# Ordering the last three groups of a two-layer graph network kernel: softmax one pair ahead, seeded first results, another share-out of the tails

## The chip, the cores and the metric

The kernel runs on one core of one Trainium2 chip. The metric is the device time of one launch in microseconds (us). The time before is the median of three runs. Beside it stands one profiled execution, whose span (first to last instruction) is what the trace is read in.

## The reference

Inputs: `x` of 128 batches x 128 tokens x 512 features, float32, an adjacency matrix `adj` (128 x 128), weights for one attention layer. Cut to what matters:

```python
# layer 0: a max over neighbours, through two einsums with the same adj
A = einsum('od,bdn->bon', adj, x);  C = A + b
x = layernorm(x + max(relu(A[:, :, None, :] + (C - A)[:, :, :, None]), axis=-1))
# layer 1: masked attention with 8 heads of 64 features, mask where adj == 0
q, k, v = split(x @ w_qkv)
p = softmax(where(adj == 0, -inf, q @ k.T * 64 ** -0.5))
o = (p @ v) @ w_proj + b_proj
x = layernorm(x + o + layernorm(o) * gamma + beta)
```

So each batch of 128 tokens passes a small matmul and a maximum, a layernorm, a q/k/v projection, scores, a softmax over 8 x 128 x 128 values, attention, an output projection, and then a "tail": an inner layernorm of o, two additions, and an outer layernorm.

## The kernel before, in words

**Tiling.** Four batches make a group (NG = 32 groups), and batches are handled in pairs (64 pairs, loop variable p). The projections of a group (512 tokens x 512 features) are done by a scheme with 7 products instead of 8 block products: operands are added up beforehand (`left_sums`, `weight_sums`) and the 7 products are combined afterwards. Class `Unit` does this for q/k of a half (`qk_unit`), for v (`v_unit`) and for the output projection (`o_unit`). A product is four matmuls of 128 x 256, each of which shows as two records in the trace. It accumulates in one of four PSUM banks b1 to b4: products 1, 6, 7 in b1, product 2 in b2, products 5 and 3 in b3, product 4 in b4. `snap(k)` copies b1 to SBUF on ScalarE after products 1, 6 and 7. `result(half, col)` adds a bank and a snap on VectorE and so makes one quarter of the output: (0,0) from b2 and snap 1, (0,1) from b3 after product 3 and snap 2, (1,0) from b4 and snap 3, (1,1) from b3 before product 3 and snap 3. Product 3 can therefore start only when (1,1) was read, and the next unit's product 5 only when (0,1) was read.

**Softmax.** `scores(b)` writes eight heads to two PSUM tiles (tags pss0 and pss1, or po and pa). `softmax_max` scales and masks them into an SBUF tile `s` (two buffers) and takes the maximum on VectorE; `softmax_exp` runs eight exponentials with sums on ScalarE; `softmax_div` divides on VectorE; `prob_transpose` transposes 32 x 32 blocks on VectorE. `prob_write` sends the result to DRAM (`hop`), and `prob_read` fetches it back with rows regrouped (`pT`, two buffers, four transfers of 128 KB), both on SyncE's (SP's) queue. `prob_move` is the three in a row. `attend(b)` multiplies with v; `attend_copy` moves the result to `oT`.

**Tails.** In the loop a pair's tail is: bias on GpSimd (`tail_bias`), statistics on VectorE (`bn_stats`, `bn_aggr`), power -0.5 on GpSimd (`finish_stats`), inner layernorm on ScalarE (`tail_inner`), three operations on GpSimd (`tail_residual`: times gamma, plus o, plus the spilled x), outer statistics, outer layernorm on ScalarE (`tail_outer`) and the store. Behind the loop this is done batch by batch (`tail_inner_one`, `tail_residual_one`, `tail_outer_one`). For some batches VectorE does it instead of GpSimd (`fused_open`, `fused_close`), and for some batches ScalarE makes the outer statistics (`scalar_stats`, `finish_scalar_stats`). The last group's projection is not a Unit: `last_project` multiplies each batch by all of w_proj into a bank that `last_seed` filled with the bias.

**What sets the order.** Everything is pinned in program order (`keep_in_program_order`), so each engine runs its instructions in the order in which the text issues them. A wait holds whatever is queued behind it on that engine. SP's queue carries all transfers of this part.

**Around the change.** With L = 127 the last batch, the loop runs p up to LAST = 60. Iteration 60 attends batches 118 and 119 (L-9, L-8) and starts the softmaxes of L-7 and L-6. What follows the loop is written out by hand: o of group 29, v of group 31 and o of group 30 (in the text `o_u`, `v_u`, `o_u`), the softmaxes of L-5 to L, the tails of the last 14 batches, and the four last projections. In that part o units are seeded with the bias (`seed`, a ScalarE copy into banks 2, 3 and 4).

Of the kernel before, what the change touches and what calls it, by code (L numbers as in the profile page):

```python
# [16 lines left out]
def kernel(  # L17
# [144 lines left out]
    class Unit:  # L162
# [25 lines left out]

        def result(self, half, col):
            bank, k = {(0, 0): (2, 1), (0, 1): (3, 2), (1, 0): (4, 3), (1, 1): (3, 3)}[half, col]  # L190
            pin(
                nc.vector.tensor_tensor(  # L192
                    self.out[half, col], self.banks[bank], self.snaps[k], ALU.add
                )
            )
# [55 lines left out]
    def finish_stats(mv, keys, eng=None, fused=0):  # L251

        n = len(keys)
        if n == 0:
            return
        sh = small.tile([P, NC], F32, tag="sh", name=f"sh_{mv.name}")
        if eng is None:
            pin(nc.vector.tensor_scalar(sh[:, :n], mv[:, :n, 0], -1.0, None, ALU.mult))
# [3 lines left out]
        if eng is None:  # L262
            tt(nc.gpsimd, sh[:, :n], sh[:, :n], rs[:, :n], ALU.mult)
        elif n > fused:

            part = slice(fused, n)
            pin(eng.tensor_scalar(sh[:, part], mv[:, part, 0], -1.0, None, ALU.mult))
            tt(eng, sh[:, part], sh[:, part], rs[:, part], ALU.mult)
# [232 lines left out]
    def o_unit(g):  # L501
# [4 lines left out]
        return Unit(f"o_{g}", o_lefts[g], tokens_stationary(wp), out)  # L506
# [11 lines left out]

    def seed(unit, bank):
        cols = slice(HE, D) if bank == 3 else slice(0, HE)  # L520
        bias = bp_bc[:, cols].unsqueeze(1).to_broadcast([P, 2, HE])
        pin(nc.scalar.copy(unit.new_bank(bank), bias))
# [37 lines left out]
    def tail_reload_one(b, place):  # L560
        rs_[b] = place
        pin(nc.sync.dma_start(out=place, in_=spill[b // 2][:, b % 2]))
# [71 lines left out]
    def stats(name, *items, eng=None, fused=0):  # L634

        mv = small.tile([P, NC, 2], F32, tag="mv", name=f"mv_{name}")
        for k, (kind, b) in enumerate(items):
            bn({"o": o_of, "z": zs.get, "y": xs.get}[kind](b), mv, k)
        finish_stats(mv, items, eng, fused)
        return mv  # L640
# [131 lines left out]
    for p in range(LAST + 1):  # L772
# [121 lines left out]
        elif p == LAST:  # L894
            second = qk_unit(g + 1, 1)
# [23 lines left out]
        if p == 1:  # L919
            weight_sums(wp, 0, HE)  # L920
        if f is not None:
            one("y", xs, f)
# [6 lines left out]

    L = B - 1  # L930
    po_pa = ("po", "pa")
    pool = nc.gpsimd
# [4 lines left out]
    before.snap(3)  # L937
    attend_copy(L - 7)
    attend(L - 6, "pa")
    attend_copy(L - 6)  # L940
    seed(o_u, 2)
    scores(L - 5)
    scores(L - 4, po_pa)
    before.result(1, 1)
    tail_inner(B // 2 - 7)
    softmax_max(L - 5)
    before.result(1, 0)
    softmax_max(L - 4)
    o_u.product(1)
    o_u.snap(1)  # L950
    o_u.product(2)
    softmax_exp(L - 5)
    seed(o_u, 4)
    o_u.result(0, 0)
    before.product(3)
    before.result(0, 1)
    tail_residual(B // 2 - 7)
    softmax_exp(L - 4, range(4))
    o_u.product(6)
    scores(L - 3)  # L960
    scores(L - 2, po_pa)
    o_u.snap(2)
    seed(o_u, 3)
    softmax_exp(L - 4, range(4, H))
    softmax_div(L - 5)
    prob_move(L - 5)
# [3 lines left out]
    softmax_max(L - 3)  # L970
    softmax_exp(L - 3, range(4))
    o_u.snap(3)
    softmax_exp(L - 3, range(4, H))
    softmax_div(L - 4)
    prob_move(L - 4)
    softmax_max(L - 2)
    o_u.result(1, 1)
    o_u.result(1, 0)
    tail_outer(B // 2 - 8)
    tail_store(B // 2 - 8)  # L980
    tail_reload(B // 2 - 6)
    wlast, room = last_load()
    for t in range(L - 9, L + 1):
        tail_reload_one(t, room[:, t - L + 9])
    v_u.product(2)
    v_u.product(1)
    v_u.snap(1)
    stats("last_1", ("o", L - 9), ("o", L - 8), eng=pool)
    softmax_exp(L - 2, range(4))
    o_u.product(3)  # L990
    o_u.result(0, 1)
    v_u.result(0, 0)
    v_u.product(6)
    v_u.snap(2)
    softmax_exp(L - 2, range(4, H))
    for t in (L - 9, L - 8):
        tail_inner_one(t)
    tail_residual_one(L - 9)
    v_u.product(5)
    v_u.product(7)  # L1000
    stats("last_2", ("o", L - 11), ("o", L - 10), eng=pool)
    tail_residual_one(L - 8, [0])
    softmax_div(L - 3)
    prob_transpose(L - 3)
    prob_write(L - 3)
    v_u.snap(3)
    v_u.product(4)
    v_u.result(1, 1)
    softmax_div(L - 2)
    prob_transpose(L - 2)  # L1010
    prob_write(L - 2)


    attend(L - 5)
# [5 lines left out]
    scores(L - 1)  # L1020
    scores(L, po_pa)
    run_sums(o_sums(NG - 2))
    o_u = o_unit(NG - 2)
    seed(o_u, 2)
    for t in (L - 11, L - 10):
        tail_inner_one(t)
    softmax_max(L - 1)
    v_u.result(1, 0)
    v_u.product(3)
    softmax_max(L)  # L1030
    softmax_exp(L - 1, range(4))
    o_u.product(1)
    o_u.snap(1)
    seed(o_u, 4)
    softmax_exp(L - 1, range(4, H))
    v_u.result(0, 1)
    o_u.product(2)
    seed(o_u, 3)
    o_u.product(6)
    o_u.snap(2)  # L1040
    o_u.result(0, 0)
    softmax_exp(L, range(4))
    tail_residual_one(L - 8, [1, 2])
    stats("last_3", ("z", L - 13), ("z", L - 12), ("z", L - 9), eng=pool)
    o_u.product(5)
    o_u.product(7)
    softmax_exp(L, range(4, H))
    o_u.snap(3)
    o_u.product(4)
    softmax_div(L - 1)  # L1050
    prob_move(L - 1)
    o_u.result(1, 1)
    softmax_div(L)
    prob_move(L)
    tail_residual_one(L - 11)
    tail_residual_one(L - 10)
    tail_outer(B // 2 - 7)
    tail_store(B // 2 - 7)
    tail_outer_one(L - 9)
    last_seed(L - 3, "b2")  # L1060
# [3 lines left out]
    attend_copy(L - 2)  # L1064
    o_u.result(1, 0)
    mv = small.tile([P, NC, 2], F32, tag="mv", name="mv_last_4")
# [111 lines left out]
```

## Time and profile before

| | before |
|---|---|
| runs, us | 1964.82, 1963.43, 1963.56 |
| median, us | 1963.56 |
| profiled execution, us | 1965.37 |
| its span, us | 1963.5 |
| mean granted TensorE clock | 0.995 |
| start of iteration 60 on TensorE | 1840.79 |
| last matmul of the trace starts | 1946.5 |
| stores and loads on SP's queue, 1838 to 1964 | 19.68 MB |

Names of engines: PE is TensorE (matmuls), PEld its weight loads, DVE VectorE, ACT ScalarE, POOL GpSimd, SP SyncE. In the rows "L74" is a line of the kernel; every matmul has L74, and every two-input elementwise operation made by the helper `tt` has L77, so rows are told apart by the tiles: `b_qk`, `b_v`, `b_o` the banks of a unit, `pss` scores, `po`/`pa` attends, `pp` last projections, `s` softmax tile, `pu` its transpose, `hop` and `pT` its way through DRAM, `u_*` snaps, `zl` and `z` tails, `mv_last` mean and variance, `rs_mv_last` and `sh_mv_last` scale and shift made of them, `wlast` the tile that holds w_proj and the reloaded x of the last batches. A number after an operation on a timeline is start and duration in us. The profiled execution is one run; its rows give durations.

### The profile page before, as it was taken

The page shows a single profiled execution, that of the slowest core. Times are in us where ns is not written, and L with a number is a line of the kernel's source. Part 1 is how long each engine was busy: PE and PEld are TensorE (multiplying, and loading weights), DVE is VectorE, ACT ScalarE, POOL GpSimd, SP SyncE. Part 2 cuts the span into 40 slices and gives each one's busy share as a digit, 9 for nine tenths or more (in the row PEclk, how much of TensorE's full clock was granted, in tenths as well). Part 3 has the DMA queues.
Part 4 walks back from the last instruction along what each step waited for, and adds up shares of the span by engine and source line. Part 5 has one row for each costly group of instructions (what it writes and reads, how often), then busy time and mean ns, then how long its engine had stood idle before and what let it go on. Part 6 is the DMA issues. An engine that isn't in the chain of part 4 may idle for free.

```text
span 1963.5 us, 33034 instructions
## 1 busy us (share of the span) xinstructions
PE 1935.3 (99%) x11533; PEld 1637.7 (83%) x11533; DVE 1561.6 (80%) x2513; ACT 1061.6 (54%) x3084; POOL 1297.2 (66%) x827
## 2 busy tenths in 40 slices
PE   9999999999999999999999999999999999999995
PEld 6888888888888888888888888888888888888873
DVE  6767878878778778788787787787887877877876
ACT  3444654655555546546555555455465555554564
POOL 6336766767666767667676667676676766676748
PEclk9999999999999999999999999999999999999998
DMA  7647557576576676675675765765756657667554
GB/s 226 171 119 189 148 175 193 156 189 173 166 196 163 167 200 161 171 186 163 188 181 161 195 162 167 207 156 168 193 158 187 175 169 193 166 168 194 141 182 139
DMA packets 445653, 341.73 MB, mean 174 GB/s; under 512 B 276912, under 2 KB 378416, under 8 KB 445488
## 3 DMA queue, kind: packets, MB, share of 16 engines
q1 hardware_dynamic: 445056, 338.85, 63.3%
q8 instruction: 91, 1.49, 0.3%
q10 hardware_dynamic: 432, 0.79, 0.1%
q14 instruction: 74, 0.61, 0.1%
HBM read 172.82 MB, written 166.72 MB: 173 GB/s over the span
## 4 chain that ended last, share of the span: by engine, by line
PE 96%; DVE 2%; POOL 1%; ACT 1%; DMA 1%; issue 0%; SPq 0%; POOLq 0%; DVEq 0%; ACTq 0%
PE b_qk L74 40%; PE b_v L74 19%; PE b_o L74 18%; PE pss L74 6%; PE po L74 6%; PE pa L74 5%; PE pp L74 0%; DMA wlast<-spill 0%; ACT s L420 0%; POOL zl L77 0%; DVE s L401 0%; DVE s L77 0%; POOL rs_mv_last L77 0%; DVE st_mv_last L248 0%; DVE pu L441 0%
## 5 line engine op out<-in xcount | busy, mean ns | idle before, releaser
L74 PE MATMUL b_qk<-s_x,wqk 128*128 128x256 f32 x2048 | 473.2, 379 | 0.2 <-DVE v L192 0.2
L74 PEld LDWEIGHTS b_qk<-s_x,wqk 128*128 128x128 f32 x2048 | 389.0, 190 | 54.1 <-DVE v L192 0.6
L420 ACT ACTIVATE s<-s,nmax 128x128 f32<-128x128 f32 x1024 | 396.2, 391 | 5.7 <-DVE nmax L413 5.7
L74 PE MATMUL b_qk<-x1T,wqk 128*128 128x256 f32 x1536 | 358.9, 383 | 0.1
L74 PEld LDWEIGHTS b_qk<-x1T,wqk 128*128 128x128 f32 x1536 | 286.6, 190 | 45.3 <-issue 1.0
L77 POOL TENSOR_TENSOR z<-z,ga_bc 128x1024 f32<-128x1024 f32 x58 | 164.7, 2839 | 169.2 <-ACT z L274 169.2
L260 POOL TENSOR_SCALAR rs_mv<-mv 128x6 f32<-128x6 f32 (+2 forms) x61 | 14.6, 239 | 380.9 <-DVE mv L249 380.9
L77 DVE TENSOR_TENSOR s<-s,rec 128x1024 f32<-128x1024 f32 x128 | 252.0, 1969 | 4.4
L186 ACT COPY u_qk<-b_qk 128x512 f32<-128x512 f32 x192 | 112.4, 585 | 245.7 <-PE b_qk L74 244.7
L74 PE MATMUL b_v<-wv,s_x 128*128 128x256 f32 x1024 | 236.9, 379 | 0.0
L74 PE MATMUL b_o<-wp,s_o 128*128 128x256 f32 x992 | 229.7, 379 | 4.0 <-POOL s_o L77 2.6
L74 PEld LDWEIGHTS b_v<-wv,s_x 128*128 128x128 f32 x1024 | 194.4, 190 | 26.6
L74 PEld LDWEIGHTS b_o<-wp,s_o 128*128 128x128 f32 x992 | 188.2, 190 | 30.7 <-POOL s_o L77 3.0
L192 DVE TENSOR_TENSOR qk<-b_qk,u_qk 128x512 f32<-128x512 f32 x256 | 168.2, 676 | 56.6 <-PE b_qk L74 44.4
L401 DVE SCALAR_TENSOR_TENSOR s<-pss,mask 128x512 f32<-128x512 f32 x256 | 164.3, 684 | 59.0 <-PE pss L74 58.8
L77 POOL TENSOR_TENSOR x<-x,be_bc 128x1024 f32<-128x1024 f32 x64 | 181.3, 2834 | 33.4 <-DVE rec L431 27.3
L192 DVE TENSOR_TENSOR v<-b_v,u_v 128x512 f32<-128x512 f32 x128 | 87.1, 681 | 136.9 <-PE po L74 132.1
L420 ACT ACTIVATION_READ_ACCUMULATOR s<-s,nmax 128x1 f32 x1024 | 194.4, 190 | 0.0
L186 ACT COPY u_v<-b_v 128x512 f32<-128x512 f32 x96 | 56.2, 585 | 235.8 <-PE b_v L74 235.8
L186 ACT COPY u_o<-b_o 128x512 f32<-128x512 f32 x93 | 54.4, 585 | 237.0 <-PE b_o L74 237.0
L74 PE MATMUL b_v<-wv,x1T 128*128 128x256 f32 x768 | 176.2, 379 | 0.0
L74 PEld LDWEIGHTS b_v<-wv,x1T 128*128 128x128 f32 x768 | 145.9, 190 | 32.2 <-issue 13.6
(121 smaller groups left out, 3398.8 us busy)
## 6 DMA issues: line engine op xcount, KB each, us to landing
hop<-pu SPq DMA_DIRECT2D x128, 512.0 KB, 3.4
pT<-hop SPq DMA_DIRECT2D x512, 128.0 KB, 3.7
spill<-x SPq DMA_DIRECT2D x64, 512.0 KB, 4.8
x<-in_x_dram SPq DMA_DIRECT2D x62, 512.0 KB, 4.4
xhop<-xt SPq DMA_DIRECT2D x248, 128.0 KB, 2.2
x1T<-xhop SPq DMA_DIRECT2D x248, 128.0 KB, 3.9
xr<-spill SPq DMA_DIRECT2D x59, 512.0 KB, 3.6
out_dram<-xr SPq DMA_DIRECT2D x58, 512.0 KB, 4.1
```

The costliest lines, as they stand in the source:

```text
L74: pin(nc.tensor.matmul(*args, **kwargs))
L77: pin(eng.tensor_tensor(dst, a, b, op))
L186: pin(nc.scalar.copy(t, self.banks[1]))
L192: nc.vector.tensor_tensor(self.out[half, col], self.banks[bank], self.snaps[k], ALU.add)
L260: pin(nc.gpsimd.tensor_scalar(rs[:, :n], mv[:, :n, 1], EPS, None, ALU.add))
L401: nc.vector.scalar_tensor_tensor(s[:, par], pss[b][par], SCALE, mask.unsqueeze(1).to_broadcast([P, NP, P]), ALU.mult, ALU.add,)
L420: nc.scalar.activation(prob[b][:, i], prob[b][:, i], AF.Exp, bias=nmax[b][:, i : i + 1], accum_out=psums[b][:, i : i + 1],)
```

## The change

The diff does five things, all of them behind the loop's iteration p = 59 but for one small tile.

1. Iteration 60 is taken out of the loop and written out. In it the scores of L-5 and L-4 follow `first.product(6)`, and both softmaxes are done there, one pair ahead of where they stood; the written-out part behind it is one pair ahead as well (scores of L-1 and L before v's unit rather than after it).
2. Results stand ahead of maxima where a bank waits for them, and a pair's write goes out ahead of the reads (`prob_out` is `softmax_div`, `prob_transpose`, `prob_write`).
3. For the two o units and the v unit of this part the quarter (0,0) is no longer a VectorE addition: ScalarE copies b1 to b2 (`relay`), product 2 accumulates on it, and ScalarE copies b2 to the output (`relayed`). The bias is seeded in b1, and b3 gets the difference of the two halves of the bias (`bd`, made once on GpSimd in iteration 1).
4. The reloads of the last ten batches are five pair loads (`tail_reload_to`) instead of ten, two of them into a buffer of `x1T` (`early`).
5. The tails are shared out anew: GpSimd makes those of L-11 to L-8, L-6, L-5 and L-4, VectorE (fused) L-7 and L-3 to L, and ScalarE makes the outer statistics of L-11, L-10, L-5 and L-4. Before, the fused ones were L-6 and L-3 to L, and ScalarE had L-11 and L-8. The negated mean of `finish_stats` is on VectorE again (before: GpSimd in this part).

```diff
+        def relay(self):
+            pin(nc.scalar.copy(self.new_bank(2), self.banks[1]))
+        def relayed(self):
+            pin(nc.scalar.copy(self.out[0, 0], self.banks[2]))
...
-            pin(eng.tensor_scalar(sh[:, part], mv[:, part, 0], -1.0, None, ALU.mult))
-            tt(eng, sh[:, part], sh[:, part], rs[:, part], ALU.mult)
+        if n > fused:
+            tt(nc.gpsimd, sh[:, part], sh[:, part], rs[:, part], ALU.mult)
...
     def seed(unit, bank):
-        cols = slice(HE, D) if bank == 3 else slice(0, HE)
-        bias = bp_bc[:, cols].unsqueeze(1).to_broadcast([P, 2, HE])
+        bias = {1: bp_bc[:, :HE], 3: bd}[bank].unsqueeze(1).to_broadcast([P, 2, HE])
...
-    for p in range(LAST + 1):
+    for p in range(LAST):
...
+            bd = const.tile([P, HE], F32, name="bd")
+            tt(nc.gpsimd, bd, bp_bc[:, HE:], bp_bc[:, :HE], ALU.subtract)
...
+    first.product(6)
+    scores(L - 5)
+    scores(L - 4, po_pa)
+    softmax_exp(L - 6, range(4))
...
+    prob_out(L - 7)
+    softmax_max(L - 5)
+    first.snap(3)
+    prob_out(L - 6)
+    first.result(1, 1)
...
+    softmax_max(L - 4)
+    first.result(1, 0)
...
+    first.product(3)
+    first.result(0, 1)
+    softmax_exp(L - 4)
+    prob_out(L - 5)
...
+    prob_out(L - 4)
...
+    o_u.product(1)
+    o_u.relay()
...
+    o_u.product(2)
+    o_u.relayed()
     scores(L - 3)
     scores(L - 2, po_pa)
+    tail_reload(LQ - 5)
+    wlast, room = last_load()
+    for q in range(3):
+        tail_reload_to(LQ - 2 + q, room[:, ds(2 * q, 2)])
+    softmax_max(L - 3)
+    softmax_max(L - 2)
+    o_u.product(6)
     o_u.snap(2)
+    softmax_exp(L - 3)
...
+    scores(L - 1)
+    scores(L, po_pa)
...
+    prob_out(L - 3)
     o_u.result(1, 1)
     o_u.result(1, 0)
+    softmax_max(L - 1)
+    stats("last_1", ("o", L - 9), ("o", L - 8))
...
+    prob_out(L - 2)
     o_u.result(0, 1)
...
+    softmax_max(L)
...
+    softmax_exp(L)
     v_u.product(5)
...
+    prob_out(L - 1)
...
     attend(L - 5)
...
+    prob_out(L)
     v_u.result(0, 1)
...
+    tail_inner_one(L - 6)
+    stat = scalar_stats(L - 11, L - 10)
+    tail_residual_one(L - 5, [0, 1])
+    fused_open(L - 7, mv[:, 0, 0:1])
+    mv = stats("last_6", ("o", L - 3), fused=1)
...
+    stat = scalar_stats(L - 5, L - 4)
+    tail_residual_one(L - 6, [0])
+    mv = stats("last_8", ("o", L - 1), ("z", L - 2), fused=1)
+    fused_open(L - 1, mv[:, 0, 0:1])
+    fused_close(L - 1)
+    tail_residual_one(L - 6, [1, 2])
+    finish_scalar_stats(stat)
+    for t in (L - 2, L - 5, L - 4):
         tail_outer_one(t)
+    mv = stats("last_9", ("o", L), ("z", L - 1), ("z", L - 6), fused=1)
+    fused_open(L, mv[:, 0, 0:1])
+    for t in (L - 1, L - 6):
+        tail_outer_one(t)
+    fused_close(L)
+    mv = stats("last_10", ("z", L), fused=1)
     tail_outer_vector(L, mv[:, 0, 0:1])
```

## The prediction

> **What bounds the kernel now.** I read the page first (busy times, 40 slices), then TensorE's own waits, the windows around the longest of them, and the chain of waits from its end.
>
> ```profile
> PE 1935.3 (99%) x11533; PEld 1637.7 (83%) x11533; DVE 1561.6 (80%) x2513; ACT 1061.6 (54%) x3084; POOL 1297.2 (66%) x827
> ```
>
> TensorE (PE) is the bound up to 1840, 94% of the span, and there nothing is left to gain without removing matmuls. The change touches only what follows the loop's iteration p = 60, whose first matmul (attend of batch L-9) starts at 1840.79. All of TensorE's waits behind that point are these:
>
> ```profile
> PE po L74 <- DMA pT<-hop: 3.7, 1, 3.7
> PE b_o L74 <- POOL s_o L77: 2.6, 1, 2.6
> ...
> PE b_o L74 <- DVE o L192: 1.0, 1, 1.0
> ...
> PE b_o L74 <- ACT b_o L522: 0.3, 1, 0.3
> ```
>
> Together 7.7 us. The first one costs more than its length, as the stretches of 2 us around it show (start:end, length, then busy us of PE, PEld, DVE, ACT, POOL, then the granted TensorE clock):
>
> ```profile
> 1928.00:1930.00 2.00, 0.73 (x14) 0.48 (x10) 1.93 (x5) 1.90 (x6) 1.83 (x3) 1.00 0.50 128
> 1930.00:1932.00 2.00, 0.00 (x0) 0.00 (x0) 1.30 (x3) 0.81 (x3) 1.68 (x5) 0.98 0.99 297
> 1932.00:1934.00 2.00, 1.54 (x15) 1.57 (x16) 0.00 (x0) 1.38 (x3) 1.73 (x4) 0.50 0.60 231
> ...
> 1938.00:1940.00 2.00, 2.00 (x5) 0.85 (x4) 0.00 (x0) 0.00 (x0) 1.53 (x2) 0.81 0.02 7
> ```
>
> After 3.73 us without a matmul the clock is 0.50 from 1932 to about 1939.3. Some 6.9 us of matmuls run at half speed: 3.4 us more. So 7.7 + 3.4 = 11.1 us of TensorE time are lost behind 1840.79. The last matmul ends at 1947.1, and 16.4 us follow it. The chain of waits names what fills them:
>
> ```profile
> 1951.30 1.28 POOL zl L77
> ...
> 1954.31 0.89 POOL rs_mv_last L77
> ...
> 1955.22 0.76 DVE z L627
> ...
> 1959.51 0.81 ACT zl L274
> ```
>
> GpSimd (POOL) makes the tail of a batch with three 128x512 operations in a row and the statistics' power in between. The end is a relay POOL, DVE, POOL, ACT, not one busy engine.
>
> **The change, part by part.** Base: the profiled execution took 1965.37 with a span of 1963.5, 1.9 around it; the median of the runs shown is 1963.56, 1.8 below that execution. I work in span time and carry the difference to the median.
>
> TensorE does the same matmuls. A product is 1.73 (8 records), a pair of attends 1.90, a pair of scores 1.98, a last projection 3.45. Behind 1840.79 come 36 products, 5 pairs of attends, 4 of scores and 4 projections: 62.3 + 9.5 + 7.9 + 13.8 = 93.5. Without any wait TensorE would end at 1840.8 + 93.5 = 1934.3.
>
> *Softmax one pair ahead.* Steps on VectorE, start to start: placing scores 1.32, maximum 1.13, reciprocal 0.22, division 1.26 alone, transpose 1.27, a result 0.61, statistics of a batch 0.83. Scores of L-5 and L-4 now sit behind first.product(6), ending at 1853.7. VectorE: v result to 1850.8; division and transpose of L-7 to 1853.8; maximum of L-5 to 1856.3; L-6 to 1860.0 (division taken as 2.2); result (1,1) to 1860.6; maximum of L-4 to 1863.1; result (1,0), two statistics, result (0,1) to 1865.9. That last result frees bank 3 for second.product(5), where TensorE arrives at 1865.8: a wait of 0.2, or 0.7 if the division takes the 2.75 shown below. Behind the waiting matmul are products 4 and 7; nobody else waits. I take 0.5. Then attends of L-7, L-6 at 1871.2: their reads are issued from 1860.4 and 1863.5 on SP's queue and land by 1868.9.
>
> The next four softmaxes: maximum of L-3 ends 1881.9; L-2 1884.3; ScalarE (eight exponentials 3.08) has L-3 ready at 1885.7, held back by snap(2) behind o_u.product(6). From 1885.7 VectorE is solid: L-3 2.75, results (1,1) and (1,0) 1.22, maximum of L-1 2.45, two statistics 1.81, L-2 2.75, result (0,1) 0.61 = 11.6, so 1897.3. TensorE reaches v_u.product(5), which needs that bank, at 1896.1. **A new wait of 1.2**; 1.7 with a lock. Behind it on PE stand v_u.7 and v_u.4.
>
> Then: L's maximum 1899.8, statistics 1901.6, L-1 written 1904.9, L 1909.3. So the reads of L-3 and L-2, behind hop(L-1) on SP's queue, land by 1911.5, against their attends at 1916.6. The reads of L-1 and L need the two pT buffers, free after attends L-3 and L-2 (1917.6, 1918.5). Four issues took 1.73 and the landing 3.33 in the trace: L lands at 1924.4, and o_u.3 + one projection + one attend (1.73 + 3.45 + 0.95) carry TensorE from 1918.5 to 1924.6. **The 3.7 us wait and the half clock go**, with a margin of 0.2 to 1. The 2.6 us wait on s_o goes too: those sums start at 1906.7, and the products needing no sum (1, 2, 4) come first, so product 6 meets them at 1911.4 against 1909.3. TensorE ends at 1934.3 + 0.5 + 1.7 + about 1 (drains at a wait, banks) = 1937.5.
>
> *Results and seeds.* Three results (0,0) leave VectorE (3 x 0.61) for a copy on ScalarE (relayed), and snap(1) becomes relay, a PSUM to PSUM copy. No row shows such a copy: between nothing beyond a snap (0.58) and twice that. It is a PSUM read of equal size, so 0.58, start to start 0.48. ScalarE has one seed fewer per o unit, so it pays one copy net, for v, beside 2.6 us of idle time there. The bias difference bd is one 128x256 subtraction on GpSimd in iteration 1, 0.65 as half of the 1.27 of a 128x512 one, hidden in GpSimd's 34% idle time; uncovered it would cost 0.65.
>
> *Loads.* Ten single loads (7.5 us on SP's queue, GpSimd waiting 4.65 for one) become five pair loads, two of them 30 us earlier. They stand in front of hop(L-5), which leaves about 2 us later; its attend is 20 us off. Cost 0.
>
> *Statistics.* The negated means (nine before, eight now) move from GpSimd (0.24 to 0.80 each) to VectorE (0.15 each). Two statistics (2 x 0.83) move to ScalarE, where one costs 1.75.
>
> *The end.* GpSimd still makes seven tails and four sums. From 1905.3 its queue is: powers and shifts of L-11/L-10 1.4, sums 5.2, then tail operations of 1.3 and powers (0.9 to 1.7) without pause. Through z of L-6: 12 tail operations for L-11, L-10, L-5, L-4 and 3 for L-6 = 19.5; seven sets of powers = 9.4 more; one wait of 1.4 for ScalarE's statistics of L-11 and L-10, which cannot start before the copy of L's attend: in all to 1942.3. Behind it the relay: three statistics and shift 2.65, power 1.35, close 0.75, statistics 0.83, power 0.95, last outer 0.6, store and end 3.2 (as in the trace, 1960.3 to 1963.5) = 10.4, 10.5 with handovers. **Span 1952.8.** TensorE's extra 1 shifts ScalarE's statistics: 1953.7. GpSimd now sets the end, not TensorE, and some of the 11.1 comes back as this wait.
>
> **A rule against the change.** Rows of the division on VectorE, and of tail operations on GpSimd:
>
> ```profile
> 1854.33 2.75 DVE L77 TENSOR_TENSOR s<-s,rec 128x1024 f32<-128x1024 f32 x1
> ...
> 1886.06 1.23 DVE L77 TENSOR_TENSOR s<-s,rec 128x1024 f32<-128x1024 f32 x1
> ...
> 1916.41 2.13 POOL L77 TENSOR_TENSOR zl<-zl,wlast 128x512 f32<-128x512 f32 x1
> ...
> 1920.37 2.26 POOL L77 TENSOR_TENSOR zl<-zl,ga_bc 128x512 f32<-128x512 f32 x1
> ```
>
> The same operation takes 1.23 while GpSimd is idle and 2.75 beside it; GpSimd's 1.27 becomes 2.13 or 2.26 beside a division. The Trainium skill, "SBUF — State Buffer", section "SBUF: two separate sides", says that VectorE with two SBUF inputs and GpSimd hold one pair of ports in turn for a whole instruction. Taken at its word, each of the five closes, the two fused opens from SBUF and the divisions of L-1 and L costs up to one operation, 9 x 1.27 = 11 us, and the gain is gone. In the trace only 3 of 25 such GpSimd operations were stretched (2.4 us in all), and closes pushed GpSimd's small shift to 0.8. I take the rows: three closes at 0.65 and small rest, 2.0. Sum: 1953.7 + 2.0 = 1955.7, less 0.2 as the three shifts no longer on GpSimd cannot be pushed: **1955.5**, 8.0 below 1963.5.
>
> **Rivals.**
> 1. *Clean end.* No pushed operations and a TensorE wait under 1: 1951 to 1953.5. For: in the trace 22 of 25 operations ran at 1.27. Against: GpSimd is now continuously busy, so every close meets it.
> 2. *TensorE waits again.* If the transposes of L-1 or L come 3 us late, or reads land at 4.5 rather than 3.3, the attend waits as long as the 3.73 of before, and the clock halves again: 3.7 + 3.4. (The wait of 2.6 left it at 1.00 in the window 1910 to 1920.) ScalarE's statistics and the GpSimd queue behind them shift with the attend; part is covered by the 6 us that the last projection is early. End 1957 to 1963. For: a margin under 1 us. Against: reads have no loads beside them any more (the pair loads are done by 1892).
> 3. *Slower: the port lock on GpSimd's last queue.* 19 operations of 128x512 stand in one row from 1906.7 (four sums, fifteen tail operations). Each 0.1 on their mean moves the end by 1.9. At 2.2, as in the stretched rows, it is 1953.7 + 19 x 0.9 = 1970.8. It decides above a mean of 2.03 (13.8 / 19 over 1.3); between 1.6 and 2.0 the time is unchanged. Against it: the mean was 1.37.
>
> **How the numbers follow.** About 0.2% (3.9 us) is what a measurement can tell here. Main course 0.60 (1953.5 to 1958.5, all faster); clean end 0.18, faster; TensorE waits again 0.14, of which 0.06 faster and 0.08 same; lock 0.08, of which 0.02 same and 0.06 slower. Faster 0.84, same 0.10, slower 0.06. Median 1963.56 - 8.0 = 1955.5. Range 1951 to 1961: it takes in the clean end, the main course and half of rival 2.
>
> **What would show it.** TensorE's clock 1.00 until its last matmul, near 1937.5; its longest wait in the last 120 us at b_v (product 5), 1 to 2 us, on VectorE's result; none over 3 us on pT. GpSimd idle less than 3 us between 1906 and 1942, the mean of its 128x512 operations under 1.45. VectorE's statistics of the last z wait for GpSimd. I am wrong in the mechanism if TensorE ends after 1942, or if GpSimd has long gaps there and the end is still near 1955; wrong in the size if the end lies over 14 us after z of L-6 is made.

## The result, and the profile after

The changed kernel takes 1959.62 us (median of 16 runs, 1958.87 to 1960.44), the kernel before 1963.9 beside it on the same chip (16 runs, 1962.67 to 1965.32). The ratio is 0.9978, with a 95% interval of 0.9970 to 0.9986: 4.3 us, or 0.22%, faster. The forecast was 8.0 us. The profiled execution took 1959.19, with a span of 1957.4.

TensorE first. The busy line of the page, then TensorE's waits behind 1838 in the trace (us in total, times, longest):

```profile
PE 1932.5 (99%) x11533; PEld 1635.9 (84%) x11533; DVE 1562.1 (80%) x2514; ACT 1065.3 (54%) x3094; POOL 1296.3 (66%) x821
```

```profile
PE b_v L74 <- DVE o L199: 0.9, 1, 0.9
PE b_o L74 <- POOL s_o L77: 0.7, 1, 0.7
PE b_qk L74 <- DVE qk L199: 0.6, 1, 0.6
```

The wait of 3.7 on pT is gone, that of 2.6 on `s_o` is 0.7, and 7.7 us of waits have become 2.2. The stretch of 10 us in which the clock halved before (its mean there was 0.66) and the one behind it, in the changed kernel (start:end, length, busy us of PE, PEld, DVE, ACT, POOL, granted clock, DMA share, GB/s):

```profile
1930.00:1940.00 10.00, 9.62 (x23) 3.99 (x21) 6.67 (x12) 5.83 (x14) 9.01 (x14) 1.00 0.14 53
1940.00:1950.00 10.00, 0.00 (x0) 0.00 (x0) 7.05 (x17) 6.90 (x14) 8.20 (x11) 0.59 0.22 80
```

TensorE keeps the clock of 1.00 to its last matmul, which ends at 1939.6; before it ended at 1947.1. So TensorE is done 7.5 us sooner, yet the span is only 6.1 shorter in this pair of profiles and the median 4.3. GpSimd's timeline shows who holds the end (start, duration, instruction, idle time before it):

```profile
1900.76 1.27 POOL L77 TENSOR_TENSOR zl<-zl,ga_bc 128x512 f32<-128x512 f32 x1 [2.47 <-ACT zl L278]
...
1904.69 2.27 POOL L77 TENSOR_TENSOR zl<-zl,ga_bc 128x512 f32<-128x512 f32 x1
...
1934.52 0.25 POOL L678 TENSOR_SCALAR de<-de 128x2 f32<-128x2 f32 x1 [0.34 <-ACT trash L669]
...
1939.92 1.71 POOL L77 TENSOR_TENSOR zl<-zl,wlast 128x512 f32<-128x512 f32 x1
...
1944.06 1.71 POOL L77 TENSOR_TENSOR zl<-zl,o 128x512 f32<-128x512 f32 x1
1945.86 1.26 POOL L77 TENSOR_TENSOR zl<-zl,early 128x512 f32<-128x512 f32 x1
```

From 1900.76 to 1947.12 GpSimd has a single gap, of 0.34. Its last product is z of L-6, and VectorE waits for it:

```profile
1947.15 0.69 DVE L255 BATCH_NORM_STATS2 st_mv_last<-zl 128x6 f32<-128x512 f32 x1 [2.50 <-POOL zl L77]
```

From there the relay to the end takes 1957.4 - 1947.1 = 10.3. The end belongs to GpSimd's queue, 7.5 us after TensorE's last matmul. The experiments ask whether that was already so before, and which terms the forecast had wrong. None of them takes back the first part of the change, the softmaxes one pair ahead, or the second or fourth, so what each of these is worth alone stays open.

**Theory A:** GpSimd's queue of tails sets the end, in both kernels; what TensorE gains there is worth nothing. **Theory B:** TensorE sets it, through the last projections. **Theory D:** part of the forecast's base was peculiar to the one profiled execution of before.

### The profile page after: what moved, and what is told of

Same layout as the page of the kernel before. It is cut to its first block, busy times and chain, and to the rows that moved or that the text cites. A ratio compares the mean times of both kernels' runs of the same rounds, so it can differ in the third digit from the quotient of the medians.

```text
span 1957.4 us, 33035 instructions
## 1 busy us (share of the span) xinstructions
PE 1932.5 (99%) x11533; PEld 1635.9 (84%) x11533; DVE 1562.1 (80%) x2514; ACT 1065.3 (54%) x3094; POOL 1296.3 (66%) x821
## 4 chain that ended last, share of the span: by engine, by line
PE 94%; DVE 3%; POOL 2%; ACT 1%; issue 0%; POOLq 0%; ACTq 0%; DVEq 0%
PE b_qk L74 39%; PE b_v L74 19%; PE b_o L74 18%; PE pss L74 6%; PE po L74 6%; PE pa L74 5%; POOL zl L77 1%; DVE s L77 0%; DVE pu L445 0%; ACT s L424 0%; DVE st_mv_last L255 0%; DVE amax L291 0%; POOL rs_mv_last L77 0%; POOL s_o L77 0%; DVE s L405 0%
```

## The experiments

Each kernel was timed beside the kernel before on the same chip. "Gain" is the median of the kernel before, run beside it, minus the kernel's own median: 4.57 for the changed kernel itself in experiment 1. The intervals of the ratios are about 0.001 (2 us) wide to each side, and the kernel before spreads over 2.5 us, so differences under 2 us rest on the traces, one of each kernel, read from the start of iteration 60 on TensorE to the end of the span: 115.76 in the changed kernel (1841.64 to 1957.4).

**1. The changed kernel once more (`c_after`).** No edit.

> The changed kernel once more, as the base of the runs beside it, and for a second profile. Both theories: a median near 1959.6 us, ratio to before 0.997 to 0.999. The profile should show again: TensorE's last matmul 17 to 18 us ahead of the end, GpSimd without a gap over 1.5 us from about 1901 to 1949 (from the span's start), three waits of TensorE behind 1840, all under 1 us.

1959.02 (8 runs, 1958.63 to 1959.41), before 1963.59, ratio 0.9975 (0.9965 to 0.9985). The result holds in this second set of runs, and the second profile shows the same three waits of TensorE (0.9, 0.7, 0.6), again only one gap of GpSimd between 1901 and 1947 (0.4), and 115.7 from iteration 60 to the end.

**2. The last projection made late (`x_pe_late`).**

```diff
     last_project(L - 1, wlast)
+    filler = psum.tile([P, 2 * P], F32, tag="pss1", name="filler")
+    for _ in range(12):
+        pe(filler, lhsT=zeros[:, :P], rhs=zeros, start=True, stop=True)
     last_project(L, wlast)
```

> The changed kernel with 12 filler matmuls of zeros (128x256, about 5.2 us) between the last two projections, so that TensorE ends about 5.2 us later and nothing else is moved. Theory A (GpSimd's queue of tails sets the end; the last projection is ready some 9 us before VectorE takes it up at 1948.8): the time is that of the changed kernel within 1 us. Theory B (the last projection still sets the end, with a fixed tail of some 17 us behind it): 4 to 5 us slower than the changed kernel.

TensorE's timeline in this kernel:

```profile
1935.54 5.34 PE L74 MATMUL filler<-zeros 128*128 128x256 f32 x24
1940.72 3.60 PE L74 MATMUL pp<-wlast,oT 128*128 128x512 f32 x8
```

The last projection ends at 1944.3, 4.7 later than in the changed kernel. Time 1959.41 (12 runs), ratio 0.9978 (0.9969 to 0.9986), span 1956.9: nothing paid. TensorE's end has at least 4.7 us of slack, which speaks against B.

**3. GpSimd relieved (`x_pool_light`).** The kernel leaves out nine of GpSimd's operations, so three batches of its output are not the layer's; it only shows what their time is worth.

```diff
-    tail_residual_one(L - 5, [0, 1])
...
-    tail_residual_one(L - 5, [2])
...
-    tail_residual_one(L - 4, [0, 1])
...
-    tail_residual_one(L - 4, [2])
...
-    tail_residual_one(L - 6, [0])
...
-    tail_residual_one(L - 6, [1, 2])
```

> The changed kernel without GpSimd's nine residual operations of L-5, L-4 and L-6 (left out: times gamma, plus o, plus x for these three batches), 9 x 1.3 = 11.7 us of its last queue. Theory A: the end moves forward until the next bound, the last projection at 1939.6 with VectorE's statistics, open, close, power, outer step and store behind it (about 10 to 12 us), so 5 to 8 us faster than the changed kernel. Theory B: within 1 us of it.

1954.84 (5 runs, 1953.57 to 1955.0), ratio 0.9951 (0.9939 to 0.9964): gain 8.75, 4.2 more than the changed kernel. A expected 5 to 8, so its lower edge is missed: of the nine operations' 12 us only 4.2 arrive, since VectorE becomes the next bound. In its timeline from 1939.94 on there is no gap until it waits 1.01 for the very last power.

```profile
1939.94 0.75 DVE L624 SCALAR_TENSOR_TENSOR z<-pp,mv_last,ga_bc 128x512 f32<-128x512 f32 x1
1940.61 0.68 DVE L77 TENSOR_TENSOR wlast<-pp,wlast 128x512 f32<-128x512 f32 x1
1941.39 0.75 DVE L632 SCALAR_TENSOR_TENSOR z<-z,rs_mv_last,wlast 128x512 f32<-128x512 f32 x1
...
1948.75 0.55 DVE L653 TENSOR_SCALAR z<-z,mv_last,rs_mv_last 128x512 f32<-128x512 f32 x1 [1.01 <-POOL rs_mv_last L77]
```

Less work on GpSimd is time, more work on TensorE is none. That is A for the changed kernel.

**4. The kernel before, a second profile (`c_before`).** No edit.

> The kernel before once more, for a second profile. The profile shown lies 1.5 to 1.8 us above the median of its kind. Theory D (how long the clock stays at half speed behind the 3.7 us wait differs from run to run): this profile has the same wait of 3.5 to 3.9 us, and where the span is 1 us or more shorter, the stretch at half clock is shorter too. Theory E (the difference lies in the first 20 us, where the clock and the first loads differ): iteration 60 starts earlier by the difference of the spans.

One run: 1963.07, span 1961.2, 2.3 shorter than the profile that the forecast was made from. Iteration 60 starts at 1840.63 (1840.79 there), so the difference lies behind it. The windows behind TensorE's wait for pT, here 4.27 long:

```profile
1930.00:1932.00 2.00, 0.22 (x2) 0.25 (x4) 0.85 (x2) 2.00 (x5) 1.52 (x3) 0.85 1.05 344
1932.00:1934.00 2.00, 2.00 (x17) 1.67 (x16) 0.71 (x1) 0.29 (x2) 1.77 (x3) 0.50 0.28 107
1934.00:1936.00 2.00, 2.00 (x4) 0.82 (x4) 1.90 (x6) 2.00 (x4) 1.84 (x4) 0.79 0.02 7
1936.00:1938.00 2.00, 2.00 (x6) 0.95 (x5) 0.45 (x2) 0.50 (x1) 1.92 (x2) 1.00 0.68 255
```

Half speed lasts 3.4 us here against 6.8 in the profile of before, after a longer pause (D had expected one of 3.5 to 3.9). TensorE's last matmul ends near 1944.8 instead of 1947.1. That is D: the stretch varies from run to run. In the profile of before the long stretch did reach the end: VectorE waits there 3.13 for a projection, and GpSimd 1.67 for VectorE. In `c_before` VectorE's wait in this place is 1.55 and GpSimd has none. The two lines, from VectorE's and GpSimd's timelines of the profile of before:

```profile
1940.27 0.70 DVE L248 BATCH_NORM_STATS2 st_mv_last<-pp 128x6 f32<-128x512 f32 x1 [3.13 <-PE pp L74]
```

```profile
1941.28 0.23 POOL L260 TENSOR_SCALAR rs_mv_last<-mv_last 128x3 f32<-128x3 f32 x1 [1.67 <-DVE mv_last L249]
```

The stretch is not all of the 2.3. Followed along GpSimd's timelines, 0.2 is there before iteration 60, 0.6 comes from a reload that GpSimd waits 4.65 for instead of 3.60 (part of it vanishes in a gap of 0.69 that `c_before` has at 1930.30), and 1.6 appears at the wait of 1.67.

**5. The kernel before without the halved clock (`x_before_warm`).** Eight filler matmuls keep TensorE at work while it waits for pT:

```diff
     attend(L - 1)
+    filler = psum.tile([P, 2 * P], F32, tag="pss1", name="filler")
+    for _ in range(8):
+        pe(filler, lhsT=zeros[:, :P], rhs=zeros, start=True, stop=True)
     attend(L, "pa")
```

> The kernel before with 8 filler matmuls of zeros (128x256, about 3.5 us) between the attends of L-1 and L, where TensorE waits 3.7 us for pT and then runs at half clock. The wait stays, its effect on the clock goes. If the clock behind that wait is worth its 3.4 us of TensorE time: 2.5 to 3.5 us faster than before. If the tail of before is held by GpSimd as that of the changed kernel is: less than 1 us.

1964.18 (13 runs), ratio 1.0000 (0.9992 to 1.0009). In the profiled run the granted clock stays at 1.00 up to the last matmul, as the windows around the place show:

```profile
1926.00:1934.00 8.00, 7.43 (x52) 5.37 (x52) 5.42 (x11) 7.06 (x17) 6.49 (x12) 1.00 0.54 174
1934.00:1940.00 6.00, 6.00 (x15) 2.66 (x14) 4.50 (x9) 1.50 (x3) 5.59 (x7) 1.00 0.23 87
```

TensorE's last matmul ends at 1943.3, and the span of 1961.3 is that of `c_before`. So the halved clock of 3.4 us, as `c_before` has it, cost the kernel before nothing: GpSimd held its end too. This is A for the kernel before. The two sets of runs spread alike as well (1963.15 to 1965.05 with the fillers, 1962.91 to 1964.98 without), so nothing says that the long stretch, which did cost 1.6 in one profile, sets the median; where the clock fell in runs without a profile isn't known.

**6. One snap moved (`x_u2`).** ScalarE's timeline in the changed kernel showed a wait that the forecast had not seen:

```profile
1899.38 0.58 ACT L186 COPY u_v<-b_v 128x512 f32<-128x512 f32 x1 [1.37 <-DVE o L199]
```

`v_u.snap(2)` writes the one buffer `u2`, which `o_u.result(0, 1)` on VectorE still reads; the inner layernorms of L-9 and L-8 stand behind it on ScalarE, and GpSimd's first tail waits for those (the 2.47 at 1900.76). The edit gives the snap the buffer `u1`:

```diff
-    v_u.snap(2)
+    v_u.snap(2, "u1")
```

> The changed kernel with v's second snap in the buffer of the first snap, which relay left unused, so that ScalarE's snap no longer waits for VectorE's result (0,1) of the o unit. In the profile that wait is 1.4 us and the inner steps of L-9 and L-8, on which GpSimd's queue starts, stand behind it. Theory A: GpSimd's first tail operation starts 1.0 to 1.6 us earlier and the end moves forward by 0.7 to 1.6 us, TensorE's wait of 0.7 us on s_o goes. Theory C (the port lock, not the start, makes GpSimd's queue late): the start moves, the end does not.

1958.65 (7 runs), ratio 0.9974 (0.9963 to 0.9984), gain 4.94. GpSimd's timeline:

```profile
1901.14 1.28 POOL L77 TENSOR_TENSOR zl<-zl,ga_bc 128x512 f32<-128x512 f32 x1 [1.55 <-ACT zl L278]
...
1927.80 0.66 POOL L269 TENSOR_SCALAR rs_mv_last<-mv_last 128x2 f32<-128x2 f32 x1
1928.54 1.01 POOL L77 TENSOR_TENSOR rs_mv_last<-rs_mv_last,mhalf 128x2 f32<-128x2 f32 x1
...
1932.36 0.67 POOL L269 TENSOR_SCALAR rs_mv_last<-mv_last 128x1 f32<-128x1 f32 x1
```

Iteration 60 starts at 1842.96 in this profile, so GpSimd's first tail comes 58.18 after it, against 59.12 in the changed kernel: 0.94 earlier. TensorE's wait on `s_o` is gone, as A expected. To the end it is 115.24 against 115.76, so about half arrives. At the first of the four sums the queue is still 1.13 earlier; from there to z of L-6 it takes 35.8 instead of 35.3, since other small instructions than before now run long beside VectorE (the last three lines; the same three take 0.22, 0.71 and 0.23 in the changed kernel). The direction is A's, the size (0.4 by the medians, 0.5 by the traces) is under A's 0.7 to 1.6 and within the spread of the runs.

**7. The statistics of the first layer in their old order (`x_order`).** The diff changed `columns` to go through its items backwards, and `columns` also serves the opening, which the forecast had called untouched. There, in the changed kernel, VectorE waits for the batch that ScalarE finishes last, and TensorE behind it:

```profile
31.59 0.69 DVE L255 BATCH_NORM_STATS2 st_mv_second<-x 128x6 f32<-128x512 f32 x1 [0.85 <-ACT x L296]
```

```profile
PE b_qk L74 <- DVE qk L199: 0.8, 1, 0.8
```

```diff
-        for k, (kind, b) in reversed(list(enumerate(items))):
+        order = enumerate(items) if items[0][0] == "y" else reversed(list(enumerate(items)))
+        for k, (kind, b) in order:
```

> The changed kernel with the statistics of layer 0 in the old order (the new helper goes through its list backwards, in the opening part too, where VectorE then waits 0.85 us for the last of four additions and TensorE 0.79 us for the result behind it, at 35.7). If that wait shifts the whole loop: 0.8 us faster than the changed kernel (1958.2), iteration 60 starts 0.8 earlier, and no wait of TensorE on qk at 35 us. Otherwise no change.

1958.69 (7 runs), ratio 0.9972 (0.9962 to 0.9983), gain 5.47, 0.9 more than the changed kernel; median against median it is 0.3. In its trace the 0.8 at `b_qk` in the first 80 us is gone, and iteration 60 starts at 1841.03 instead of 1841.64 (1840.79 and 1840.63 in the two profiles of before). The trace settles the cause: a part of the change that its description hides costs some 0.6 in the opening.

**8. The last GpSimd tail given to VectorE (`x_fuse6`).** Cut:

```diff
-    mv = stats("last_5", ("o", L - 7), ("o", L - 6), fused=1)
+    mv = stats("last_5", ("o", L - 7), ("o", L - 6), fused=2)
...
-    tail_inner_one(L - 6)
...
     fused_open(L - 2, mv[:, 0, 0:1])
+    fused_open(L - 6, mv6[:, 1, 0:1])
...
-    tail_residual_one(L - 6, [0])
...
     fused_close(L - 1)
-    tail_residual_one(L - 6, [1, 2])
+    fused_close(L - 6)
```

> The changed kernel with the tail of L-6 made by VectorE (fused, as L-7's) in place of GpSimd, three GpSimd operations (3.9 to 4.7 us with what holds them up) fewer and about 2.1 us more on VectorE, which waits 2.5, 2.0 and 1.2 us in that part. Theory A (GpSimd's queue sets the end): 2 to 4 us faster than the changed kernel, with the statistics of z of L-6 no longer waiting for GpSimd. Theory B (TensorE): within 1 us, or slower by VectorE's 2 us.

1957.63 (5 runs, 1957.4 to 1957.87), ratio 0.9966 (0.9954 to 0.9979), gain 6.53, 2.0 more than the changed kernel, or 1.4 median against median; from iteration 60, 114.4 against 115.76. A had expected 2 to 4, so this is its lower edge or less. The statistics of the last z no longer wait (VectorE's timeline):

```profile
1944.81 0.74 DVE L632 SCALAR_TENSOR_TENSOR zl<-zl,rs_mv_last,early 128x512 f32<-128x512 f32 x1
1945.59 0.69 DVE L255 BATCH_NORM_STATS2 st_mv_last<-zl 128x6 f32<-128x512 f32 x1
```

VectorE's wait of 2.50 in the changed kernel is gone, for 2.2 us of work (open 0.74, sum 0.69, close 0.74), of which the first two fall before 1939.4, and the end moves by 1.4 to 2.0. GpSimd has gaps of 0.70 and 1.33 here before its last powers, and VectorE now runs from 1940.13 to its last power without a gap, as in experiment 3.

**9. The negated means back on GpSimd (`x_sh_pool`).** In `finish_stats`, for the last ten statistics:

```diff
+            if eng is None:
-            pin(nc.vector.tensor_scalar(sh[:, part], mv[:, part, 0], -1.0, None, ALU.mult))
+                pin(nc.vector.tensor_scalar(sh[:, part], mv[:, part, 0], -1.0, None, ALU.mult))
...
         tt(nc.gpsimd, rs[:, :n], rs[:, :n], mhalf.to_broadcast([P, n]), ALU.pow)
...
+            if eng is not None:
+                pin(eng.tensor_scalar(sh[:, part], mv[:, part, 0], -1.0, None, ALU.mult))
```

> The changed kernel with the negated means of the last ten statistics back on GpSimd (as before the change), behind the power. Theory A (GpSimd's queue sets the end): each costs 0.24 or more on it, eight of them, six in front of the last z of GpSimd, and one in the relay behind it: +1.2 to +2.5 us against the changed kernel (1959.0). Theory B (TensorE sets the end): under 0.3 us, since TensorE waits for none of them after 1915.

1962.47 (13 runs, 1961.94 to 1963.61), ratio 0.9993 (0.9985 to 1.0001), gain 1.37: 3.2 lost, about 70% of the whole gain, by eight operations on 128x1 to 128x4 elements. From iteration 60 (1842.87) to the end (1961.7) it is 118.8, 3.1 more. GpSimd's timeline:

```profile
1943.12 0.80 POOL L274 TENSOR_SCALAR sh_mv_last<-mv_last 128x2 f32<-128x2 f32 x1
1944.00 0.20 POOL L77 TENSOR_TENSOR sh_mv_last<-sh_mv_last,rs_mv_last 128x2 f32<-128x2 f32 x1
1944.15 1.27 POOL L77 TENSOR_TENSOR zl<-zl,wlast 128x512 f32<-128x512 f32 x1
...
1947.84 0.80 POOL L274 TENSOR_SCALAR sh_mv_last<-mv_last 128x1 f32<-128x1 f32 x1
```

A expected 1.2 to 2.5 and B under 0.3. The size is above A's, because three of the eight take 0.80 and not 0.25: each falls beside a close of VectorE (`fused_close`, at 1931.61, 1943.07 and 1947.79 in its timeline). The reader can see the trade: the `zl` behind it takes 1.27 here and 1.71 at the same place in the changed kernel (1939.92 above). In these rows one close pushes one GpSimd instruction, whichever is there.

**10. Two of the outer statistics on VectorE (`x_two_stats`).**

```diff
-    stat = scalar_stats(L - 5, L - 4)
...
-    finish_scalar_stats(stat)
-    for t in (L - 2, L - 5, L - 4):
+    for t in (L - 2,):
         tail_outer_one(t)
-    mv = stats("last_9", ("o", L), ("z", L - 1), ("z", L - 6), fused=1)
+    mv = stats("last_9", ("o", L), ("z", L - 1), ("z", L - 6), ("z", L - 4), ("z", L - 5), fused=1)
...
-    for t in (L - 1, L - 6):
+    for t in (L - 5, L - 4, L - 1, L - 6):
```

> The changed kernel with the outer statistics of L-5 and L-4 on VectorE instead of ScalarE (so ScalarE makes two, not four). Theory A: VectorE waits 2.5 us for the last z of GpSimd in the changed kernel, and the two statistics (2 x 0.83) fill that wait; the last power has five columns instead of three (+0.2): +0.2 us, between -0.2 and +0.8. Rival C (VectorE is as late as GpSimd, so the share of ScalarE is what gains): +1.2 to +1.7 us.

1961.74 (13 runs, 1960.74 to 1962.76), ratio 0.9988 (0.9980 to 0.9997), gain 2.10: 2.5 lost, where A said 0.2 and the rival 1.2 to 1.7. From iteration 60, 117.55 against 115.76, so 1.8. Both reasons were wrong. VectorE does take the two statistics within its wait: z of L-6 is done at 1948.37, and its statistics begin at 1948.41. What is longer lies behind, 12.0 from z of L-6 to the end instead of 10.3. Five of the last six stores are now issued between 1953.69 and 1956.22, and the transfers fill the engines (windows of 2 us; the last two columns are the DMA share and GB/s):

```profile
1954.00:1956.00 2.00, 0.00 (x0) 0.00 (x0) 0.80 (x3) 1.77 (x3) 0.82 (x2) 0.50 0.73 269
1956.00:1958.00 2.00, 0.00 (x0) 0.00 (x0) 0.00 (x0) 0.00 (x0) 0.00 (x0) 0.50 1.02 377
```

In the changed kernel the stores of L-5 and L-4 leave at 1949.33, before these; from the issue of the last store to the end it is 3.0 there and 4.2 here. So 1.2 of the 1.7 behind z of L-6 is the last store; the rest lies ahead of its issue, where the power of five columns takes 1.20 and not 0.88. By the trace, ScalarE's statistics gain by an early store, not by relief of VectorE; no run moved the stores alone.

**11. The relays undone (`x_relay_off`).** Part 3 of the change reversed; cut:

```diff
-    o_u.relay()
+    o_u.snap(1)
...
-    o_u.relayed()
+    o_u.result(0, 0)
+    seed(o_u, 4)
...
-    v_u.relayed()
+    v_u.result(0, 0)
```

> The changed kernel with part 3 of the change undone: the three quarters (0,0) are again additions on VectorE (0.61 each), snap(1) is again a copy to SBUF, and the o units' bias is seeded in banks 2, 3 and 4 as before. Theory A (GpSimd's queue of tails sets the end, from its start near 1900.8 on): these additions matter only as far as they delay the statistics of L-9 and L-8 or the softmaxes in front of them, so 0 to +0.7 us against the changed kernel (1959.0), TensorE's wait on b_v 0.9 to 1.5. Theory B (VectorE's row of softmaxes sets TensorE and TensorE the end): each addition is paid, +1.2 to +1.8 us, and TensorE's waits behind 1880 grow by as much.

1959.76 (13 runs, 1959.24 to 1960.89), ratio 0.9979 (0.9971 to 0.9988), gain 4.08, 0.5 less than the changed kernel. TensorE's waits behind 1838 in this kernel:

```profile
PE b_o L74 <- ACT b_o L527: 1.1, 1, 1.1
PE b_v L74 <- DVE o L199: 1.0, 1, 1.0
PE b_qk L74 <- DVE qk L199: 0.6, 1, 0.6
PE b_v L74 <- DVE v L199: 0.4, 1, 0.4
```

They are 3.1 against 2.2, GpSimd's first tail comes 59.17 after iteration 60 (59.12 before the edit), and the end 116.3 against 115.76. This is what A expected: TensorE's extra 0.9 costs about half, and the three additions are not paid one by one. Whether the half is the additions or the third seed is not told apart.

**12. Three edits together (`best1`).** Experiments 6, 7 and 8 in one kernel.

> The changed kernel with three edits together: the statistics of layer 0 in their old order, v's second snap in the buffer u1, and the tail of L-6 on VectorE. Alone they gave -0.3, -0.4 and -1.4 us against the changed kernel (1959.0). Theory A: they act at different places (opening, start of GpSimd's last queue, its end), so they add up to about -2.1: 1956.9, between 1956.2 and 1957.7. Rival: the earlier start of GpSimd's queue only makes it wait for ScalarE's statistics or for the attends, so 1957.3 to 1957.7 as with the last edit alone.

1956.35 (5 runs, 1956.21 to 1957.63), ratio 0.9963 (0.9951 to 0.9976): gain 7.49, 2.9 more than the changed kernel, against 0.4 + 0.9 + 2.0 = 3.3 by the gains of the single edits. All five runs are below the fastest of the 24 of the changed kernel (1958.63), though not run beside them. This is the fastest version here. Within the part behind iteration 60 the earlier start adds little: 114.2 against 114.4 with the last edit alone. That is what the rival said of these two edits; the sum of all three, 2.7 by the medians, lies in A's range. The profiled execution was the slowest of the five: its iteration 60 starts at 1841.70, against 1841.03 in experiment 7. It has 3.4 us of half clock in the opening, from 18.4 to 21.8, which experiment 7 lacks, and a wait that experiment 7 lacks too (TensorE's waits, first 80 us):

```profile
PE pa L74 <- DMA x<-in_x_dram: 0.9, 1, 0.9
```

## Why the prediction was right, and where its size was off

**Right: the mechanism on TensorE.** The waits came out at 0.9 for `b_v` (1.2 foreseen), 0.6 for `b_qk` (0.5 foreseen) and none on pT; the clock stayed at 1.00. TensorE ended at 1939.6, where the forecast had 1937.5; 0.85 of that is the later start of iteration 60, and since the waits are those foreseen in sum (2.2), the other 1.3 is matmul time that the sum of 93.5 had too small. The `s_o` wait was not foreseen to survive; it is 0.7.

**Right: GpSimd's queue is the new bound, and its length.** One gap of 0.34 (under 3 foreseen), a wait of VectorE for the last z of 2.50, and a relay of 10.3 (10.5 foreseen). Its nineteen operations of 128x512 behind 1911.8 have a mean of 1.33 (sixteen at 1.27, then 1.60, 1.71 and 1.71), under the 2.03 that the slower rival needed. The allowance of 2.0 for the lock, taken from the rows and not from the rule's full price of 11, was right in kind: behind 1911.8 the pushed instructions (those that run longer beside a VectorE operation than alone) lost 1.5 (0.3, 0.4 and 0.4 on the three long ones, 0.3 on a power). But two pushes of 1.0 stand ahead of that, beside the divisions of L-1 and L (the 2.27 at 1904.69, and an instruction of 128x2 that takes 1.21 at 1909.62); the forecast had named these divisions and counted closes alone. It is 3.5 in all. The copy from PSUM to PSUM, which no row had shown, takes 0.57 (0.58 foreseen), in ScalarE's timeline:

```profile
1893.33 0.57 ACT L191 COPY b_v<-b_v 128x512 f32<-128x512 f32 x1 [1.83 <-PE b_v L74]
```

**Off: the sum, 4.1 us too fast.** The forecast was 1955.5 as a median, with the span also at 1955.5; measured were 1959.62 and 1957.4. Three terms make the 4.1.

1. *The base, 1.8, and 0.4 for the changed kernel's own profile.* "I work in span time and carry the difference to the median" took 8.0 off the median of before. But that execution lay 1.8 above the median, and experiment 4 finds most of the excess where the change takes effect: 1.6 at the half clock of 6.8 us instead of 3.4, and 0.6 at a reload. Both are gone in the changed kernel, and a stretch of the shorter kind is worth nothing (experiment 5). So the excess was counted as a saving that a median run never had to give: the mis-sized term is the base, 1963.5 where a run at the median has a span of some 1961.7. The changed kernel's median lies 0.4 above its profile, which has no half clock in the opening; four other profiles do (last section).
2. *The opening, 0.85.* "The change touches only what follows the loop's iteration p = 60" overlooked `reversed` in `columns`. Iteration 60 starts 0.85 later, and experiment 7 shows the cause of some 0.6 of it.
3. *The start of GpSimd's queue.* The forecast let the powers of L-11 and L-10 begin at 1905.3, six operations of 1.3 behind a first tail at 1897.5. They came at 1909.62, and the first sum at 1911.85 instead of 1906.7. Of these 5.15, 0.85 is the opening, 2.4 a late first tail (0.9 of it the buffer wait of ScalarE in experiment 6; the rest was not taken apart), and 1.9 the two pushes by divisions. Behind the first sum 3.0 came back: ScalarE's statistics were waited for 0.34 and not 1.4, TensorE's extra 1 (0.9 in the sum) did not reach this queue, and the other sizes were 1.1 too large. So 1.2 was left at z of L-6, less 0.2 for the shorter relay.

1.8 + 0.4 + 0.85 + 1.0 is 4.1, within rounding. The range of 1951 to 1961 held the result, but partly by luck: the lateness of 5.15 at the first sum was met by 3.0 of errors the other way.

**Wrong as a story: "GpSimd now sets the end, not TensorE".** In `c_before` it already did, and experiment 5 speaks for the same in the median run; only in the one profile whose half clock lasted 6.8 us did TensorE reach the end. That is why 11.1 us of lost TensorE time were never the measure of what could be won, although the absolute sum along GpSimd's queue did not depend on it. Measured along that queue, `c_before` against the changed kernel, both from the start of iteration 60: GpSimd's first tail at 57.8 and 59.1, its last z done at 111.0 and 105.5, the end at 120.6 and 115.8. Between first tail and last z lie 53.2 and 46.4 us, and two things make the 6.8. One is a wait for a single reload, in the trace of `c_before`, that the pair loads removed:

```profile
1904.65 1.27 POOL L77 TENSOR_TENSOR zl<-zl,wlast 128x512 f32<-128x512 f32 x1 [3.60 <-DMA wlast<-spill]
```

With another small gap the idle time is 4.3 against 0.3. The other is the negated means, about 3 by their rows (six of them, with the steps between), and experiment 9, which puts them back, loses 3.1. I had costed the pair loads at nothing and looked only at SP's queue, though I named GpSimd's 4.65 beside it; and I left the means with no sum of their own. Against these stand the later start (1.3), the longer way from the last z to the end (0.7) and the opening (1.0): 6.8 - 1.3 - 0.7 - 1.0 = 3.8, the difference of the two spans. No run undid the pair loads alone, so that share is read from the trace and not shown by an experiment; nor was it tried what the loads and the means give without the new order of the softmaxes, whose earlier projections may be what lets the queue run without a gap.

**The rivals.** The clean end did not come: the pushed instructions took 3.5 us of GpSimd's time. TensorE did not wait again. The lock as a slower outcome stayed far from its threshold.

## What to carry to other kernels

Lost time on the busiest engine is worth only what its last result is late for: find the queue that is contiguous up to the end, and price a change along that queue, waits for loads and one-column operations included. When the profiled execution lies above the median, ask which stretch made it so before carrying a saving over, above all if the change removes that stretch. Read a helper that the diff alters in every place that calls it.

## What the runs showed of the hardware

Wherever the granted clock halved between TensorE's first and last matmul in the fourteen profiles here, it did so for 3.41 us or for twice that. In the profile of before it is 0.50 from 1931.93 to 1938.76 (6.83 us), in `c_before` from 1931.41 to 1934.82 (3.41), and in the openings of `x_u2`, `x_sh_pool`, `x_two_stats` and `best1` for 3.4 each, between 18.3 and 22.7. The longer idle time (4.27 against 3.73) had the shorter stretch. Three windows, of the profile of before, of `c_before` and of `best1` (columns as above):

```profile
1931.93:1938.76 6.83, 6.30 (x21) 3.45 (x22) 3.02 (x6) 4.15 (x7) 6.26 (x9) 0.50 0.39 149
```

```profile
1931.41:1934.82 3.41, 3.04 (x18) 2.23 (x19) 1.46 (x3) 1.70 (x4) 3.00 (x7) 0.50 0.34 132
```

```profile
14.98:18.39 3.41, 1.52 (x10) 0.89 (x9) 0.60 (x3) 1.87 (x3) 3.04 (x5) 1.00 1.06 375
```

The Trainium skill, "TensorE: Matmul & The Clock Gate", section "Part 1: The HAM clock gate (the 'warmup' mystery)", says that the gate watches activity in windows of 3.4 us that run freely, whatever the kernel does, and opens after a busy one. The lengths agree with one window and with two. In `c_before` the first window at half clock held 3.04 us of matmuls and the clock came back; in the profile of before it held 2.88 and did not. No run here set where the windows fall, so that this decides is the page's and not shown. The last line is the 3.41 us ahead of the half clock in `best1`: TensorE was busy for 1.52 of them, and its longest idle time there was 1.83, so the clock halved without an idle time anywhere near 3.4.

A VectorE operation pushes one GpSimd instruction at a time, and how far goes with the VectorE operation, not with the size of GpSimd's. Beside a close a shift of 128x2 elements went from 0.25 to 0.80 (experiment 9) and a 128x512 operation from 1.27 to 1.71; beside a division a power of 128x2 went from 0.71 to 1.73 and a 128x512 operation from 1.27 to 2.27. On the closes it shows too: 0.75 alone and 1.75 at 1932.97 in the changed kernel.

The opening moves the start of iteration 60 from run to run. Among kernels with the changed kernel's opening it was 1841.6 to 1842.0 in four profiles without a wait of TensorE for x. With such a wait (0.7 to 1.3 us) it was 1841.2 and 1841.5 in the two that kept the clock at 1.00, and 1842.9 to 1843.0 in the three that had the 3.4 us of half clock. So a single profile can start its last part over 1 us late or early for no reason in the edit, which is why the last part was read from iteration 60 on.
